# Gathers of the last token group in rows of three, each row behind the landing of the one before

## The chip, the cores and the metric

The kernel runs on one core of a Trainium2 chip. The metric is the device time of one execution in microseconds (us). Engines are named as in the profile: PE is the matrix engine (PEld its weight loads), DVE the vector engine, ACT the scalar engine, POOL the GpSimd engine, SP the sync engine, which here only issues DMAs.

## The reference, cut to what matters

Two transformer layers with pre-normalisation run over 2048 tokens of 128 channels. Each layer is an attention and a mixture of experts. The change lies in the second layer's attention, which for each query takes the 64 latest keys and 32 more that an index score picks:

```python
x = x + _L0_attn_ref(_layernorm(x), ...)     # 16 heads over all 2048 keys
x = x + _L0_ffn_ref(_layernorm(x), ...)      # 16 experts, 4 of them weighted in
x = x + _L1_attn_ref(_layernorm(x), ...)     # sparse attention, below
x = x + _L1_ffn_ref(_layernorm(x), ...)      # shared and routed experts
# in _L1_attn_ref
c_kv = x @ W_dkv
I = jnp.einsum('bths,h->bts', relu(einsum(q_i, k_i)), idx_w)
I = jnp.where(local[None], jnp.inf, I)       # the latest LW = 64 keys always
I = jnp.where(causal[None], -jnp.inf, I)
_, idx = jax.lax.top_k(I, 96)
key_c = (c_kv @ W_uk)[bi, idx]
value = (c_kv @ W_uv)[bi, idx]
kr_sel = (x @ W_kr)[bi, idx]                 # turned by rotary angles of the rank in the top k
attn = softmax(scores)
out = einsum(attn, value) @ W_out
```

So each of the 2048 queries has 32 key rows that only its own scores name, and these rows must be fetched one by one by index.

## The kernel before, in words

The tokens stand in 16 tiles of 128, in four groups of four tiles. The first layer's attention (`run`, from L422) is one long pipeline over 32 units, eight for each group of queries. When the eight units of a group are done, the rest of the network for that group, `follow(g)`, is a generator: `experts0`, `attention1`, `experts1`. For groups 0 to 2 it is drawn upon in small pieces by `advance`, so that its instructions stand between those of the next group's units. For group 3 there is no next group: at L503 `self.alone` is set, and `follow(3)` (tiles 12 to 15) runs by itself until the kernel's end. This is the tail, from about 2450 us on.

In `attention1` the compressed keys of the group (32 columns) and its rotary keys (32 columns) go to `table` in DRAM, one row of 64 floats (256 bytes) for each token. Then, for each tile n:

- `index_scores(n)` (L792): PE products, ACT relu and DVE sums make the score vector v (128 queries by up to 1984 keys).
- `choose(n)` (L824): four rounds on DVE of max, max_index and match_replace give 32 indices for each query in ix, which L842 turns into ixT. Then come 32 gathers, `gather(g)`: each is one indirect DMA issued by POOL (L853) that fetches, for one column of ixT, 128 rows of the table into slot 2·(g mod 16) + g div 16 of the tile kv, which has 32 slots. kv has three buffers, so tile 15's gathers write where tile 12's were.
- `queries(n)` (L866): the queries, their softplus and their rotation; eight small loads of the window's keys, issued by SP.
- `attend(n)` (L913): DVE rotates the 32 key columns of kv in two halves (L97, L100, L103, L104, all from the helper `rotate`). The first half reads slots 0 to 15, that is gathers 0 to 7 and 16 to 23; the second half the others, so it needs the last gather. PE transposes the result (L932), makes the scores (L942, L950, L956); then softmax (L962 to L974), the transposes of the weights (L983), the values (L991, L998), and the output product (L1012), added to xr at L1013.

While another group runs (`alone` false), the gathers are put in a list, `pay` issues one or two at a time between other work, and the branch at L847 puts them into rows of three: once three have been issued, POOL first copies one element column of each of the three landed slots into a small tile `at` (L850), which can only be done when those gathers have landed, and then issues the next. In the last group (`alone` true) that branch is not taken; L862 issues all 32 gathers of a tile one after the other. The list `issued` is made once for each group, so it runs on over the group's four tiles.

The order of the program in the tail is written at L1030 to L1042: index_scores and choose of tiles 12 and 13, then index_scores and choose of 14 beside queries and attend of 12, the same for 15 beside 13, then queries and attend of 14 and of 15. The framework plans the final order on each engine from this program order and its own estimate of when things are ready; instructions given to `keep_in_program_order` (the gathers, the copies, the first two steps of a rotation) stay in the order in which they are written. Each engine then runs its instructions strictly in that order. After `attend(15)` comes `experts1` for the group, which begins with the layernorm of all four tiles, and the output.

Of the kernel before, what the change touches and what calls it, by code (L numbers as in the profile page):

```python
# [106 lines left out]
class Program:  # L107
# [617 lines left out]
    def attention1(self, sc, g):  # L725
# [58 lines left out]
        gathers, issued, vs, chosen, qTs = [], [], {}, {}, {}  # L784

        def pay(us):

            for _ in range(min(len(gathers), max(1, round(us / 1.8)))):
                gathers.pop(0)[1]()
            return us  # L790
# [33 lines left out]
        def choose(n):  # L824

            v = vs.pop(n)
            us = v.shape[1] / 950 + 0.1
            ix = sm.tile([P, RK], U32, tag="ix", name=f"ix{n}")  # L830
            ixT = sm.tile([P, RK], U32, tag="ixT", name=f"ixT{n}", bufs=4)
            kv = sm.tile([P, RK, 64], F32, tag="kv", name=f"kv{n}", bufs=3)
            for r in range(RK // 8):
                m8 = sm.tile([P, 8], F32, tag="m8", name=f"m8_{n}_{r}")
                nc.vector.max(m8, v)
                yield pay(us)
                nc.vector.max_index(ix[:, 8 * r : 8 * r + 8], m8, v)
                yield pay(us)
                if r < RK // 8 - 1:
                    nc.vector.match_replace(v, m8, v, GONE)  # L840
                    yield pay(us)
            nc.vector.transpose(ixT, ix)  # L842

            def gather(g):
                def go():

                    if not self.alone and len(issued) == 3:  # L847
                        at = sm.tile([P, 3], F32, tag="at", name=f"at{n}_{g}")
                        for i, slot in enumerate(issued):
                            tc.keep_in_program_order(nc.gpsimd.tensor_copy(at[:, i : i + 1], slot))  # L850
                        issued.clear()
                    tc.keep_in_program_order(
                        nc.gpsimd.indirect_dma_start(  # L853
                            out=kv[:, 2 * (g % 16) + g // 16, :], out_offset=None, in_=table[0 : P * (n + 1), :],
                            in_offset=bass.IndirectOffsetOnAxis(ap=ixT[:, g : g + 1], axis=0),
                        )
                    )
                    issued.append(kv[:, 2 * (g % 16) + g // 16, 0:1])
                return go

            gathers.extend((n, gather(g)) for g in range(32))
            while self.alone and gathers:  # L862
                gathers.pop(0)[1]()
            chosen[n] = kv
# [381 lines left out]
```

## Time and profile before

| | |
|---|---|
| runs shown: median (lowest to highest) | 2804.27 us (2803.74 to 2807.57), 3 runs |
| profiled execution: time / span | 2803.35 us / 2801.6 us |
| mean granted clock of PE over the span | 0.942 |
| busy, of the span: PE / DVE / ACT / POOL | 91% / 60% / 64% / 24% |
| DMA_INDIRECT at L853, whole kernel | 512, 506.3 us busy, 989 ns mean |
| of these in the tail | 128, first start 2576.6 us, last start 2744.9 us |
| COPY at L850, whole kernel | 378 (groups 0 to 2 only), 77.8 us busy, 211 ns mean |
| other POOL instructions from 2480 us on | none |

The span is the time from the first instruction to the last on the core; the execution's own time is 1.75 us longer. The busy shares are means over stages with different limits: over the first 2400 us PE is nearly always busy, while in the tail, in the last two or three of forty equal slices of the span, PE is at five to seven tenths and POOL at seven. A row in a timeline gives the start, the duration, the engine, the line and operation, what is written from what, and in brackets the idle time before and the instruction or transfer that ended it.

### The profile page before, as it was taken

Reading aid. Unit: us, or ns where it says so; the run is one execution under the profiler, and the core shown is the slowest. Engines: PE = TensorE matmul, PEld = TensorE weight load, DVE = VectorE, ACT = ScalarE, POOL = GpSimd, SP = SyncE. Lnnn points to the kernel's source line nnn. Section 1 sums busy time; section 2 is a strip of 40 time slices with the busy share of each in tenths; the row PEclk is TensorE's granted clock in tenths of the full one; section 3 lists DMA queues with packets and bytes.
Section 4 is the critical chain, followed back from the end, with each engine's and each line's share of the span. In section 5 each row is a group of like instructions: output and inputs, shape, how many; then the busy total and the mean of one; then the engine's idle time right before and its main releaser. Section 6 shows DMA issues by size and latency. Waiting matters only on the chain. (4 is left out here: it accounts for less than half of the span.)

```text
span 2801.6 us, 39304 instructions
## 1 busy us (share of the span) xinstructions
PE 2538.6 (91%) x13452; PEld 1170.6 (42%) x13452; DVE 1670.8 (60%) x4650; ACT 1789.8 (64%) x4192; POOL 671.3 (24%) x964
## 2 busy tenths in 40 slices
PE   6999999999989999999989999999989999975566
PEld 3444444434434444434334444444433444442344
DVE  7655554565664454566685455466687654288863
ACT  3777778866666776766666677755665677533343
POOL 2111110000166610000166630000055460001771
PEclk9999999999999999999999999999999999986566
DMA  4322221111111111111121111111011120100111
GB/s 134 88 61 61 57 61 46 44 43 50 30 43 48 48 37 55 49 45 38 33 48 43 48 33 59 42 43 48 25 38 37 37 49 16 63 23 12 26 26 38
DMA packets 98103, 127.79 MB, mean 46 GB/s; under 512 B 31344, under 2 KB 49776, under 8 KB 97904
## 3 DMA queue, kind: packets, MB, share of 16 engines
q1 hardware_dynamic: 81520, 108.48, 13.8%
q0 software_dynamic: 16384, 16.81, 2.9%
q8 instruction: 106, 1.74, 0.3%
q14 instruction: 93, 0.76, 0.1%
HBM read 115.26 MB, written 9.96 MB: 45 GB/s over the span
## 5 line engine op out<-in xcount | busy, mean ns | idle before, releaser
L340 ACT ACTIVATE neg<-neg,mx 128x512 f32<-128x512 f32 x1024 | 729.8, 714 | 305.3 <-DVE neg L329 296.6
L329 DVE TENSOR_SCALAR_CACHE_REDUCE neg<-pa 128x512 f32<-128x512 f32 x1024 | 657.7, 686 | 428.1 <-PE pa L323 423.4
L390 ACT ACTIVATE e<-pb 128x512 f32<-128x512 f32 x1024 | 550.4, 595 | 293.0 <-PE pb L386 280.1
L384 PE MATMUL pb<-q,kb 64*128 64x512 f32 x2048 | 638.8, 628 | 8.5 <-DVE t_q L302 5.2
L323 PE MATMUL pa<-ka,q 64*128 64x512 f32 x2048 | 597.7, 621 | 21.9 <-ACT e L390 15.0
L853 POOL DMA_INDIRECT kv<-table,ixT x512 | 506.3, 989 | 425.3 <-DVE v L804 266.9
L399 PE MATMUL po<-e,ckv 128*64 128x512 f32 x2048 | 511.7, 612 | 0.0
L323 PEld LDWEIGHTS pa<-ka,q 64*128 64x128 f32 x2048 | 245.2, 190 | 227.0 <-issue 101.7
L303 POOL TENSOR_TENSOR q<-t_q 128x512 f32<-128x512 f32 x32 | 40.8, 1274 | 1206.3 <-DVE t_q L302 1106.7
L384 PEld LDWEIGHTS pb<-q,kb 64*128 64x128 f32 x2048 | 225.4, 190 | 210.8 <-issue 106.1
L386 PE MATMUL pb<-mrow,onesb 64*128 64x512 bf16 x1024 | 252.5, 383 | 6.8 <-ACT mrow L375 6.8
L399 PEld LDWEIGHTS po<-e,ckv 128*64 128x64 f32 x2048 | 126.9, 137 | 301.0 <-issue 283.6
L340 ACT ACTIVATION_READ_ACCUMULATOR neg<-neg,mx 128x1 f32 x1024 | 192.3, 188 | 0.0
L802 PE MATMUL pi<-kiT,qiT 64*128 64x512 f32 (+4 forms) x320 | 110.0, 610 | 26.1 <-DVE v L804 14.7
L386 PEld LDWEIGHTS <-onesb 64*128 64x128 bf16 x1024 | 69.2, 96 | 127.4 <-issue 119.6
L418 DVE SCALAR_TENSOR_TENSOR xr<-pp,rs,xr 128x128 f32<-128x128 f32 x256 | 72.2, 344 | 82.6 <-PE pp L415 69.4
L850 POOL COPY at<-kv 128x1 f32<-128x1 f32 x378 | 77.8, 211 | 174.3 <-DMA kv<-table,ixT 168.8
L721 DVE SCALAR_TENSOR_TENSOR hb<-thb,zb 128x512 f32<-128x512 f32 x64 | 44.3, 692 | 113.2 <-ACT zb L719 113.1
L808 DVE SCALAR_TENSOR_TENSOR v<-rl,iw_sb,v 128x512 f32<-128x512 f32 (+4 forms) x120 | 76.4, 642 | 51.1 <-ACT rl L807 46.7
L966 ACT ACTIVATE e<-pl,mx 128x208 f32<-128x208 f32 x128 | 54.3, 429 | 81.1 <-DVE mx L963 79.5
L303 POOL TENSOR_TENSOR kst<-t_k 128x512 f32<-128x512 f32 x32 | 41.0, 1283 | 264.0 <-DVE t_k L302 168.2
L962 DVE TENSOR_REDUCE mx<-pl 128x2 f32<-128x416 f32 x64 | 37.7, 590 | 100.3 <-PE pl L956 99.9
(276 smaller groups left out, 2859.0 us busy)
## 6 DMA issues: line engine op xcount, KB each, us to landing
ka<-kd SPq DMA_DIRECT2D x128, 256.0 KB, 3.6
kb<-kd SPq DMA_DIRECT2D x128, 256.0 KB, 3.7
wb<-in_wx SPq DMA_DIRECT2D x64, 192.0 KB, 2.4
kd<-kst SPq DMA_DIRECT2D x32, 256.0 KB, 2.3
kv<-table,ixT POOLq DMA_INDIRECT x512, 2.5
wd<-in_wx SPq DMA_DIRECT2D x40, 192.0 KB, 3.7
csk<-in_cs SPq DMA_DIRECT2D x4, 512.0 KB, 6.7
csq<-in_cs SPq DMA_DIRECT2D x4, 512.0 KB
```

The costliest lines, as they stand in the source:

```text
L303: nc.gpsimd.tensor_tensor(dst, t[:, 0, :], t[:, 1, :], ALU.add)
L323: nc.tensor.matmul(ps[h], q[rows, qt * P : qt * P + P], k[rows, :], start=True, stop=True)
L329: nc.vector.tensor_scalar(t, ps[h], -1.0, None, ALU.mult, ALU.min, accum_out=mx[at])
L340: nc.scalar.activation(t, t, AF.Exp, bias=mx[at], scale=-1.0, accum_out=su[at])
L384: nc.tensor.matmul(ps[h], k[rows, c], q[rows, :], start=True, stop=False)
L386: nc.tensor.matmul(ps[h], self.onesb[rows, :], mrow[rows, :], start=False, stop=True)
L390: nc.scalar.activation(e[:, h, :], ps[h], AF.Exp)
L399: nc.tensor.matmul(self.pos[u][cols, :], self.ckv[:, kb, :], e[:, h, :], start=(kb == 0), stop=(kb == NT - 1))
L802: nc.tensor.matmul(pi[:, : hi - lo], qiT[h // 2][rows, q], kiT[rows, lo:hi], start=True, stop=True)
L808: nc.vector.scalar_tensor_tensor(v[:, lo:hi], rl[:, : hi - lo], w["iw"][:, h : h + 1], v[:, lo:hi], ALU.mult, ALU.add)
L850: tc.keep_in_program_order(nc.gpsimd.tensor_copy(at[:, i : i + 1], slot))
L853: nc.gpsimd.indirect_dma_start(out=kv[:, 2 * (g % 16) + g // 16, :], out_offset=None, in_=table[0 : P * (n + 1), :], in_offset=bass.Indire ...
```

## The change

One condition falls. The branch that makes rows of three was taken only while another group ran beside; now it is taken in the last group as well:

```diff
@@ -844,7 +844,7 @@
             def gather(g):
                 def go():
 
-                    if not self.alone and len(issued) == 3:
+                    if len(issued) == 3:
                         at = sm.tile([P, 3], F32, tag="at", name=f"at{n}_{g}")
                         for i, slot in enumerate(issued):
                             tc.keep_in_program_order(nc.gpsimd.tensor_copy(at[:, i : i + 1], slot))
                         issued.clear()
```

What follows in `go` (the gather itself and `issued.append`) is as it was. The 128 gathers of the tail get the copies before the 4th, the 7th and so on: 42 times, three copies each. The rows run on over the borders of tiles, since 32 is not a multiple of three. Nothing of groups 0 to 2 is changed, and no value that the kernel computes.

## The prediction

> **What bounds the kernel now.** I read the page's slices first, then the gathers' own line in the tail, then the timelines of POOL and DVE there. The slices say where to look:
>
> ```profile
> PE   6999999999989999999989999999989999975566
> POOL 2111110000166610000166630000055460001771
> PEclk9999999999999999999999999999999999986566
> ```
>
> The edit touches only the last group, which runs alone. There PE is idle three to five tenths, so the 91% of the whole span says nothing about it, and POOL, at 24% overall, is at seven tenths for two slices of 70 us. The line of the gathers, for the window from 2480 us on:
>
> ```profile
> L853 POOL DMA_INDIRECT kv<-table,ixT x128: 942/947/3062, 2576.6 to 2744.9; - x128
> ...
>   DVE v L804: 255.5, 1
>   issue: 40.1, 123
> ...
> DMA to landing us min/median/max: 2.3/2.4/4.5
> ```
>
> 128 gathers start over 168.3 us. POOL waited once for the first (255.5 us, nothing to do yet) and otherwise nearly only for its own issue: 40.1/123 = 0.33 us between one and the next. The timelines of POOL and of DVE at the end of the tail:
>
> ```profile
> 2700.58 0.94 POOL L853 DMA_INDIRECT kv<-table,ixT  x1 [0.30 <-issue]
> 2701.83 0.95 POOL L853 DMA_INDIRECT kv<-table,ixT  x1 [0.30 <-issue]
> 2705.70 0.94 POOL L853 DMA_INDIRECT kv<-table,ixT  x1 [2.92 <-issue]
> 2706.94 0.95 POOL L853 DMA_INDIRECT kv<-table,ixT  x1 [0.30 <-issue]
> ...
> 2744.92 0.95 POOL L853 DMA_INDIRECT kv<-table,ixT  x1 [0.30 <-issue]
> ```
> ```profile
> 2704.75 0.21 DVE L842 STREAM_TRANSPOSE ixT<-ix 128x32 uint32<-128x32 uint32 x1
> ...
> 2745.76 0.69 DVE L97 TENSOR_TENSOR w<-kv,cs 128x512 f32<-128x512 f32 x1 [1.44 <-DMA kv<-table,ixT]
> ...
> 2747.77 0.68 DVE L97 TENSOR_TENSOR w<-kv,cs 128x512 f32<-128x512 f32 x1
> ```
>
> A gather every 1.25 us, four tiles in one unbroken train; the only gap, 2.92 us at 2705, is tile 15's train waiting for its indices (L842). The last gather starts at 2744.92 and lands 2.4 us later, at 2747.3; attend(15)'s second rotation, which needs it, starts at 2747.77. From there 53.8 us of attend(15) and experts1 lead to the end of the span. So POOL's train sets the end of the tail to within half a microsecond: whatever is added to it comes out at the end, but for the 2.6 us of the gap above the usual 0.30.
>
> **What the change adds.** Nothing is removed. 128 gathers get floor(127/3) = 42 rows of copies. What such a row costs is shown by the earlier groups, which run the very code (POOL timeline, group 0):
>
> ```profile
> 758.26 0.95 POOL L853 DMA_INDIRECT kv<-table,ixT  x1 [0.31 <-issue]
> 759.21 0.48 POOL L850 COPY at<-kv 128x1 f32<-128x1 f32 x2
> 760.61 0.18 POOL L850 COPY at<-kv 128x1 f32<-128x1 f32 x1 [0.93 <-DMA kv<-table,ixT]
> 760.94 0.97 POOL L853 DMA_INDIRECT kv<-table,ixT  x1
> 762.22 0.95 POOL L853 DMA_INDIRECT kv<-table,ixT  x1 [0.30 <-issue]
> 763.47 0.95 POOL L853 DMA_INDIRECT kv<-table,ixT  x1 [0.30 <-issue]
> ```
>
> The third gather starts at 758.26; the last copy waits for its landing, 2.35 us later; the next gather starts at 760.94. The step is 2.68 us where it would be 1.25: 1.43 more. The next row starts 763.47 + 2.79 later, 1.54 more. Two of the three copies run while the third transfer is under way, so they are free; the price is landing plus one copy plus its step to the next gather: 2.4 + 0.18 + 0.15 - 1.25 = 1.48 us with the tail's median landing.
>
> Over all rows of groups 0 to 2 whose step holds nothing but copies (123 in the POOL timelines) the median step is 2.85 and the mean 3.05 without the four above 4.5 us; other gathers step by 1.30 in the mean. That makes 1.55 to 1.75. Those groups ran beside key loads at 40 to 50 GB/s, the tail's train makes 26 GB/s in all; but the tail's gathers are disturbed just as often (mean step (2744.92 - 2576.58 - 2.62)/127 = 1.305 against an undisturbed 1.25). Ends: 1.43 (the best-placed row above) and 1.79 (mean row start to row start of 5.70, less three steps of 1.305). I take 1.60, between the tail's own landing and the busier groups' mean. Sum: 42 x 1.60 = **67.2 us** on POOL, ends 60.1 and 75.2.
>
> A page has a price for the same wait: the Trainium skill, "DMA: Bandwidth & Descriptors", section "Anatomy of one DMA — SWDGE (gpsimd) path", puts a DMA issued by GpSimd at 2.0 us plus bytes/436e3; for 32 KB that is an estimate of 2.08 us. By it a row would cost 1.16 us and the rows 48.7; the trace's 2.4 us decides.
>
> **What waits behind.** Behind a waiting copy on POOL stand only gathers; POOL has no other work from 2480 us on. Those who wait for the gathers are the rotations on DVE, and behind them in DVE's order parts of choose. By 1.305 a gather and 1.60 a row, a tile's train is 32 x 1.305 + 10.67 x 1.60 = 58.8 us. It ends at 2635.4 for tile 12, 2694.2 for 13, 2753.0 for 14.
> - Tile 12's second rotation, before at 2622.13 after a stall of 5.38, waits until about 2636.5, 14.4 later. choose(14) behind it, done at 2651.8 before, is done at 2666.2; POOL wants it at 2694.2. 28 to spare.
> - Tile 13's second rotation moves from 2674.05 to 2695.3; choose(15) from 2704.96 to 2726.2, wanted at 2753.0. 27 to spare, so the gap of 2.92 before tile 15 is gone: **-2.6 us**.
> - attend(14) starts its second rotation at 2754.1 instead of 2714.77; with queries(15), which ended at 2744.3, that work took 29.6 us and is done by 2783.7, before tile 15's last landing. Hidden.
> - kv's buffer for tile 15 is free when attend(12) has read it, some 30 us after its rotation: by about 2667, before 2753.0.
> - The eight loads of the window keys are SP's and aren't queued behind anything that waits here: 0. The three-column tile `at` is only written, by POOL in order: 0.
>
> **At the end.** The last gather starts at 2576.6 + 127 x 1.305 + 42 x 1.60 = 2809.5 and lands at 2811.9. The second rotation starts there, 64.1 us after its 2747.77 (the 0.45 of slack is used up). The first half and its transposes will then be long done: before, the second half's transposes started at 2750.50, 0.64 after their rotation's end at 2749.86, behind the first half's work: **-0.6**. But PE will have stood idle before. In the same place for tile 14 the granted clock was 0.57 from 2710 to 2715 and 1.00 from 2715 to 2720: after a pause PE runs some 3.7 us (the sixteen query transposes from 2710.70) at half speed. attend(15) had paid that on its query transposes; now it pays on the second half's work: 3.7 us that do 1.85 us of it, **+1.9** (0 if the first half keeps PE warm, 4 if softmax's pauses are lengthened too).
>
> Sum: 67.2 - 2.6 - 0.5 - 0.6 + 1.9 = **65.4 us**. The profiled execution would go from a span of 2801.6 to 2867.0 and from 2803.35 to 2868.8. It was 0.9 below the median of the runs shown, so against the median: 2804.3 + 65.4 = 2869.7, say **2870 us**. With the ends of the row price and of the clock: 60.1 - 3.7 + 0 = 56 to 75.2 - 3.7 + 4 = 76, so 2860 to 2880.
>
> **Rivals.**
> 1. *The slack swallows three tiles.* If the trains of tiles 12 to 14 were hidden behind choose, only tile 15's 10.67 rows would count: 10.67 x 1.6 = 17, so 2821. For it: DVE is above nine tenths from 2580 to 2600, and it made the 2.92 gap. Against it: one gap of 2.92 in 168 us is no slack. Chance 0.05.
> 2. *DVE's order starves POOL.* The framework plans anew with the slower POOL; were choose(15) put wholly behind attend(13) (rotation at 2695; 27 us of attend, for tile 14 2712.76 to 2739.51; 37 us of choose, for tile 15 2667.84 to 2704.96), its indices would come at 2759 instead of 2726, 6 us after POOL wants them; with choose(14) likewise and rotations mis-set by a row or two, 15 to 35 us more: 2885 to 2905. For it: the order before had a stall of 5.38 because a rotation was put too early. Against: 27 us of room, twice. Chance 0.11.
> 3. *Not slower: the wait was there anyway.* If gathers beyond three in flight only queued behind one another, holding them back would cost nothing, and the long ones (up to 3.06 us) might go: at most 128 x (1.305 - 1.25) = 7 us of gain, minus the gap's 2.6 that would reappear, 2800 to 2804. It decides from the point where a landing comes within the next issue, 1.25 us after its start; the trace has none below 2.2, and the landing doesn't grow along the unbroken train (median 2.4, against 2.5 in all). Chance 0.04.
> 4. *The edit does nothing*: `issued` is appended to in both cases, so it reaches three in the last group; nothing for it, under 0.01, counted with 3.
>
> **How the numbers follow.** The forecast has 0.80: 2870, its own range 2860 to 2880. Range for eight in ten: 2857 to 2886, which reaches a little below the ends and to the near end of rival 2. A change within 0.2% (5.6 us) can't be told from none here. Slower: 0.80 + 0.11 + 0.05 = 0.96; rival 3 is split, 0.02 same and 0.02 faster.
>
> **What would show it.** 504 copies at L850 in all, 126 of them after 2570 us; rows of 5.3 to 5.7 us in the tail's POOL timeline, the last copy of each ended by a landing; the last gather's start near 2809 with no gap before tile 15; the second rotation of tile 15 ended by that landing; some 54 us from there to the end. I'd be wrong if the tail's landings in rows of three were clearly shorter than 2.3 us or the mean row above 5.8, if POOL waits for L842 in tile 14 or 15, or if something other than kv releases attend(15).

## The result and the profile after

| | before | after |
|---|---|---|
| median (lowest to highest) | 2804.01 us (2802.11 to 2807.57), 4 runs | 2874.0 us (2871.22 to 2878.28), 4 runs |
| ratio, 95% interval | 1 | 1.0247 [1.0229, 1.0264] |
| profiled execution: time / span | 2803.35 / 2801.6 us | 2878.28 / 2876.5 us |

The change makes the kernel 70.0 us slower, where +65.4 was forecast (2870). The profiled execution of after is the slowest of its four, so its span shows a difference of 74.9.

The 40 slices of after, on its page:

```profile
PE   6999999999989999999989999999899999763546
POOL 2111100000366600000456500000344620006660
```

POOL's work in the tail was two slices at seven tenths; it is three at six. It works less densely for longer, and PE in the last slices is at three to six tenths. The gathers' line L853 from 2480 us on, and then the copies' line L850 in the same window:

```profile
L853 POOL DMA_INDIRECT kv<-table,ixT x128: 940/947/3067, 2580.5 to 2813.9; - x128
...
  issue: 14.8, 48
  DMA kv<-table,ixT: 11.6, 38
...
DMA to landing us min/median/max: 2.3/2.4/4.5
```
```profile
L850 POOL COPY at<-kv x126: 173/184/732, 2585.1 to 2812.3; 128x1 f32<-128x1 f32 x126
...
  DMA kv<-table,ixT: 46.2, 46
```

The 126 copies are there, and POOL sat idle 46.2 us ahead of them for landings. A landing takes what it took before, 2.4 us in the median: holding gathers back has not made them quicker. The train, first start to last, is 233.4 us where it was 168.3. POOL's timeline at the border to tile 15 and at the end of the train (start, duration, what, and in brackets the idle time before and its releaser):

```profile
2757.05 0.34 POOL L850 COPY at<-kv 128x1 f32<-128x1 f32 x2
2758.55 0.18 POOL L850 COPY at<-kv 128x1 f32<-128x1 f32 x1 [1.16 <-DMA kv<-table,ixT]
2759.24 0.97 POOL L853 DMA_INDIRECT kv<-table,ixT  x1 [0.51 <-issue]
...
2809.92 0.94 POOL L853 DMA_INDIRECT kv<-table,ixT  x1 [0.30 <-DMA kv<-table,ixT]
2810.87 0.36 POOL L850 COPY at<-kv 128x1 f32<-128x1 f32 x2
2812.31 0.18 POOL L850 COPY at<-kv 128x1 f32<-128x1 f32 x1 [1.08 <-DMA kv<-table,ixT]
2812.64 0.97 POOL L853 DMA_INDIRECT kv<-table,ixT  x1
2813.91 0.94 POOL L853 DMA_INDIRECT kv<-table,ixT  x1 [0.31 <-issue]
```

Tile 15's first gather starts at 2759.24, 0.51 us after the copy before it: the gap of 2.92 is gone. The row at 2809.92 is as in groups 0 to 2: two copies free, the third 2.39 us after its gather's start, the next gather 2.72 after it. DVE's timeline for attend(15), after and then before:

```profile
2816.43 0.69 DVE L97 TENSOR_TENSOR w<-kv,cs 128x512 f32<-128x512 f32 x1 [12.86 <-DMA kv<-table,ixT]
...
2830.71 0.20 DVE L971 RECIPROCAL ri<-su 128x8 f32<-128x8 f32 x1 [1.07 <-ACT e L966]
...
2843.43 0.29 DVE L1013 TENSOR_TENSOR xr<-xr,pj 128x128 f32<-128x128 f32 x1 [12.52 <-PE pj L1012]
```
```profile
2758.97 0.20 DVE L971 RECIPROCAL ri<-su 128x8 f32<-128x8 f32 x1 [1.07 <-ACT e L966]
...
2771.69 0.29 DVE L1013 TENSOR_TENSOR xr<-xr,pj 128x128 f32<-128x128 f32 x1 [12.52 <-PE pj L1012]
```

DVE stood still for 12.86 us until the last landing released the second rotation. From there to the reciprocal it is 14.28 us, where it was 11.20 (2758.97 less 2747.77); from the reciprocal to L1013 12.72 in both. The 74.9 us of the two spans:

| stretch | before | after | more | forecast |
|---|---|---|---|---|
| start of the span to the tail's first gather | 2576.6 | 2580.5 | +3.9 | 0 |
| first gather to tile 15's second rotation | 171.2 | 236.0 | +64.8 | +64.1 |
| of it the rows, (233.4 - 165.7) / 42 each | | 1.61 | +67.7 | +67.2 |
| rotation to reciprocal (L971) | 11.20 | 14.28 | +3.1 | +1.3 for the three |
| reciprocal to the addition (L1013) | 12.72 | 12.72 | 0 | |
| addition to the end of the span | 29.9 | 33.1 | +3.2 | |

165.7 is the train of before without the excess of its gap, 168.34 - 2.62; it is the base for every price of a row below.

### The profile page after: what moved, and what is told of

It reads as the page before. It is cut to its first block, busy times and chain, and to the rows that moved or that the text cites. A ratio compares the mean times of both kernels' runs of the same rounds, so it can differ in the third digit from the quotient of the medians.

```text
span 2876.5 us, 39470 instructions
## 1 busy us (share of the span) xinstructions
PE 2549.5 (89%) x13452; PEld 1181.5 (41%) x13452; DVE 1672.1 (58%) x4650; ACT 1790.3 (62%) x4192; POOL 696.0 (24%) x1090
## 5 line engine op out<-in xcount | busy, mean ns | idle before, releaser
L853 POOL DMA_INDIRECT kv<-table,ixT x512 | 504.6, 986 | 416.1 <-DVE v L804 267.0
L850 POOL COPY at<-kv 128x1 f32<-128x1 f32 x504 | 104.2, 214 | 211.7 <-DMA kv<-table,ixT 207.9
L932 PE MATMUL ptr<-ident,kv 128*128 128x128 f32 x256 | 45.8, 322 | 101.6 <-DVE kv L104 57.3
```

The lines of the kernel that those rows point to most:

```text
L853: nc.gpsimd.indirect_dma_start(out=kv[:, 2 * (g % 16) + g // 16, :], out_offset=None, in_=table[0 : P * (n + 1), :], in_offset=bass.Indire ...
```

## The experiments

The theory (T): the landing wait costs about 1.6 us for each row, and because POOL's train sets the end, every row comes out there. The rivals: slack swallows the rows of tiles 12 to 14 (R1), DVE's order starves POOL (R2), or the wait was there anyway (R3). The experiments ran on three chips, and this matters: the unchanged kernel of before takes 2807.87 us (10 runs) on the first, much as in the runs of the result (2804.01, their chip is not on record), but 2908.86 (20 runs) on the second and 2920.26 (25 runs) on the third. A total is therefore set only beside before's on its own chip. Most expectations had counted from 2804; on the second and third chip none of those totals came out, not even as a difference from before there (e1 to e4 and e10 to e12), and these runs are read by their trains of gathers. The tail's timelines can be compared across chips where nothing disturbs them (the train of after is 235.4 us on the first chip and 236.2 on the third); what disturbs them is shown under rows in tile 15 alone.

### The same kernel again: e5 (first chip), e9 (third chip)

The kernel of after itself.

> The changed kernel as it is, for a second profile. The train of gathers, first start to last start, should again be 231 to 236 us; the start of the train may differ by some microseconds with what lies before it. The stretch from tile 15's second rotation to the end of the span was 60.1 us; if part of it is the phase in which the matrix engine's clock rises in the last experts, it lies anywhere from 56 to 61.

> The changed kernel as it is, beside the other three. Where the matrix engine is fed in time during an unbroken train: 65 to 75 us above the kernel before, as seen twice. On a chip where the unbroken train is accompanied by matrix instructions that come late (as in the first four runs, where the kernel before took 2909 us), rows should relieve that: the train of about 235 us again, but no more than some 10 us above the kernel before, since there the one-copy kernel, whose train is 17 us longer, was 14 us above it.

On the first chip 2877.62 us (4 runs), ratio 1.0265 [1.0236, 1.0294]: the result repeats. The profile's train runs 235.4 us from 2577.6; rotation to reciprocal is 14.28 once more (as in e4, e9 and e12, within 0.01), but from the reciprocal to the addition it is 11.42 instead of 12.72, and from the addition to the end 30.2 instead of 33.1. On the third chip the train is nearly the same, 236.2 us with no gap, yet the kernel takes 2914.12 (10 runs) against 2920.26, ratio 0.9977 [0.995, 1.0005]: no difference that can be told. In its own stretch the change costs what it did on the first chip, so before must lose about as much in the tail there; no profile of before on that chip shows where.

### What a row is made of: e7, e1, e2 and e11

Rows of one (e7, first chip); one copy for each row of three (e1, second chip); rows of three copied three gathers late, so that nothing has to be waited for (e2 on the second, e11 on the third chip). The edits to after:

```diff
-                    if len(issued) == 3:
+                    if len(issued) == (1 if self.alone else 3):
```
```diff
-                        for i, slot in enumerate(issued):
+                        for i, slot in enumerate(issued[2:] if self.alone else issued):
```
```diff
-                    if len(issued) == 3:
+                    if len(issued) == (6 if self.alone else 3):
...
-                        for i, slot in enumerate(issued):
+                        for i, slot in enumerate(issued[:3]):
...
-                        issued.clear()
+                        del issued[:3]
```

> The changed kernel, but rows of one in the last group: 127 rows, each gather waits for the one before. By the price of a row, 1.48 to 1.6 us: 188 to 203 us, less 2.6, and 3 to 6 for the matrix engine: 2992 to 3010.

> The changed kernel, but in the last group only the third slot of a row is copied: 42 copies in the tail instead of 126, the wait for the third landing stays. If the landing sets the price of a row (about 1.6 us), the two other copies run in its shadow and the time stays at that of the changed kernel, 2870 to 2878 us. Rival: if the copies' own work on POOL sets it, two thirds of the added time go: some 43 of 65 us, so about 2828.

> The changed kernel, but in the last group a row's copies stand behind the issue of the next row: the same three copies in a row, of gathers that were issued at least three issues (3.75 us) before and, with a landing of 2.4 us, have landed. If the wait for the landing is the price, it goes, and what is left is the copies' own time, no longer in a shadow: three of 0.15 to 0.2 us and a step, 0.5 to 0.8 us a row, 41 rows, 20 to 33 us, less 2.6 for the gap before tile 15: 2822 to 2838. Rival, that POOL turning from a gather to a copy and back costs by itself: near 2870.

> Copies one row behind, once more: 41 rows of copies that wait for nothing. In the first look the step with three such copies was 1.53 us against 1.25 to 1.28 without. If the wait for the landing is nearly all of the price: 41 x 0.28 = 11 us, less 2.6, and 0 to 3 for the matrix engine: 2812 to 2817 where the kernel before takes 2804. If the copies themselves were the price: near 2870.

| | chip | time, ratio to its before | train | price of a row |
|---|---|---|---|---|
| e7, 127 rows of one | first | 3056.71, 1.0892 [1.0861, 1.0923] | 423.2 | (423.2 - 165.7) / 127 = 2.03 |
| e1, 42 rows, one copy | second | 2923.05, 1.0046 [1.0024, 1.0067] | 252.0 | (252.0 - 165.7) / 42 = 2.05 |
| e2, 41 rows late | second | 2892.63, 0.9933 [0.9912, 0.9954] | 181.2 without two waits for L842 | 0.38 |
| e11, 41 rows late | third | 2914.42, 0.9991 [0.9965, 1.0017] | 183.6 without two such waits | 0.44 |

Three copies without a wait cost about 0.4 us, with the wait 1.6: three quarters of the price is the landing. Both late runs lie between the 0.28 that e11 expected and the 0.5 to 0.8 of e2. Two expectations missed in the price itself. The rows of one came out above 3010, because a lone copy makes a row dearer than three copies do, 2.03 against 1.61; e1, expected at the price of after, shows the same on another chip, so taking copies away saves nothing. POOL's timeline in e7:

```profile
2702.01 0.98 POOL L853 DMA_INDIRECT kv<-table,ixT  x1 [0.47 <-issue]
2704.68 0.18 POOL L850 COPY at<-kv 128x1 f32<-128x1 f32 x1 [1.70 <-DMA kv<-table,ixT]
2705.34 0.98 POOL L853 DMA_INDIRECT kv<-table,ixT  x1 [0.47 <-issue]
```

The copy starts 2.67 us after the gather, and the next gather 0.47 after the copy's end; in the row of three shown for after these are 2.39 and 0.15. The medians over all rows are 2.60 and 0.47 in e7, 2.55 and 0.47 in e1, 2.41 and 0.14 in after. Why, the runs don't show.

### Half as many rows: e3 (second chip), e10 (third chip)

```diff
-                    if len(issued) == 3:
-                        at = sm.tile([P, 3], F32, tag="at", name=f"at{n}_{g}")
+                    if len(issued) == (6 if self.alone else 3):
+                        at = sm.tile([P, 6], F32, tag="at", name=f"at{n}_{g}")
```

> The changed kernel, but rows of six in the last group: 21 rows instead of 42, 126 copies as before. A price for each row, whatever it holds: 21 x 1.6 = 34 us, less 2.6, and 1 to 6 us for a colder matrix engine at the end: 2836 to 2843. Rival, a price for each copy: near 2870.

> Rows of six in the last group (21 rows, 126 copies), once more. Train: 127 x 1.305 + 21 x 1.6 = 199 us (200.1 in the first look). Where nothing else is late: 31 us less 0.5 and 1 to 6 for the matrix engine, 2836 to 2843 beside 2804. A price for each copy instead would give near 2870.

The trains are 200.1 and 201.5 us: (200.1 - 165.7) / 21 = 1.64 and 1.70 a row, with twice as many copies in each. The price goes by rows, not by copies or gathers, as T has it. In time rows of six beat before on both of these chips: 2875.74 against 2908.86, ratio 0.988 [0.9863, 0.9898], and 2874.26 against 2920.26, 0.9851 [0.9803, 0.9899]. They were not run on the first chip; an estimate from the trains, less the gap of 2.6, is 2807.9 + 21 x 1.64 - 2.6 = 2840, slower than before.

### Rows in tile 15 alone: e4 (second chip), e12 (third chip)

```diff
-                    if len(issued) == 3:
+                    if (not self.alone or n == NT - 1) and len(issued) == 3:
...
-                    issued.append(kv[:, 2 * (g % 16) + g // 16, 0:1])
+                    if not self.alone or n == NT - 1:
+                        issued.append(kv[:, 2 * (g % 16) + g // 16, 0:1])
```

> Rows of three in the last tile alone (10 rows), tiles 12 to 14 in one unbroken train as before the change. If every row of the train comes out at the end: 10 x 1.6 = 16 us, less half a microsecond of slack, and 1 to 6 us for the matrix engine: 2820 to 2827. Rival, that the rows of tiles 12 to 14 were hidden behind other work and only the last tile's count: near 2870.

> Rows of three in tile 15 alone (10 rows), once more: 10 x 1.6 = 16 us, less 0.5, and 1 to 6 for the matrix engine: 2820 to 2827 where the kernel before takes 2804, if every row comes out at the end. If only the last tile's rows counted, near 2870.

This was to decide between T and R1 by the total, and by the total it decides nothing: 2908.2, ratio 1.0006 [0.9976, 1.0035], and 2912.73, 0.9971 [0.9947, 0.9995]. The trains tell why. That of e4 is 227.4 us, and two waits that before, as profiled, doesn't have stand in it. POOL's timeline of e4, from the last gather of tile 13 on:

```profile
2688.53 0.95 POOL L853 DMA_INDIRECT kv<-table,ixT  x1 [0.30 <-issue]
2714.92 0.95 POOL L853 DMA_INDIRECT kv<-table,ixT  x1 [25.44 <-DVE ixT L842]
...
2777.16 0.94 POOL L853 DMA_INDIRECT kv<-table,ixT  x1 [19.30 <-issue]
```

POOL waits 25.44 us for tile 14's indices and 19.30 before tile 15's. Without these (each less the usual 0.30), 227.4 - 25.1 - 19.0 = 183.3: tile 15's rows added 17.6. Tile 15's own 31 steps give 15.1: 2832.76 - 2777.16 = 55.6 us, less 31 x 1.305. The list `issued` starts empty at tile 15 here, so there are 10 rows, and 10 x 1.6 = 16. The waits come from elsewhere, which PE's timeline in the same kernel shows, while POOL still gathers and just after (L957 there is L956 of after; the edit adds a line):

```profile
2676.41 0.37 PE L957 MATMUL pl<-kr,qT 64*32 64x128 f32 x1 [2.43 <-issue]
2679.20 0.37 PE L957 MATMUL pl<-kr,qT 64*32 64x128 f32 x1 [2.43 <-issue]
2682.01 0.37 PE L957 MATMUL pl<-kr,qT 64*32 64x128 f32 x1 [2.43 <-issue]
...
2696.01 1.10 PE L957 MATMUL pl<-kr,qT 64*32 64x128 f32 x15 [0.33 <-issue]
```

Matmuls of 0.37 us follow one another every 2.8 us, each after 2.43 us of waiting for nothing that the profile shows; some 7 us after the last gather of the train has been issued, fifteen of them run within 1.10. DVE's timeline of e4 has the consequence:

```profile
2696.09 1.09 DVE L963 TENSOR_REDUCE mx<-pl 128x2 f32<-128x416 f32 x2 [36.99 <-remote]
...
2714.45 0.20 DVE L842 STREAM_TRANSPOSE ixT<-ix 128x32 uint32<-128x32 uint32 x1
```

DVE stands still for 36.99 us ahead of the max that reads those products; attend(12) is late by that, the rest of choose(14) stands behind it in DVE's order, and POOL waits for choose(14). In e12 the two waits are 28.63 and 22.49 us. In before and after on the runs shown, in after on the third chip (e9) and in e1 on the second, no such runs of steps stand in the tail, and in e8 on the first chip neither, though its train is unbroken; with rows of six (e3, e10) there are some, of up to 1.15 us of waiting each. So on the second and third chip an unbroken train goes with late instructions on PE, and rows of three go without; that fits before being slower there and after not. Before itself was not profiled on these chips, so for it this is argued.

### Choose first: e8 (first chip)

Could before be made faster instead? Here DVE's order in the tail is written out, choose(14) ahead of attend(12), and kv has a fourth buffer. The edit to before:

```diff
-            for m in range(n, n + 4):
-                if m < n + 2:
+            with tc.manual_schedule(engines={mybir.EngineType.DVE}):
+                for m in range(n, n + 2):
                     yield from index_scores(m)
                     yield from choose(m)
-                else:
-                    yield from beside(1, index_scores(m), queries(m - 2))
-                    yield from beside(3, choose(m), attend(m - 2))
+                yield from beside(1, index_scores(n + 2), queries(n))
+                yield from choose(n + 2)
+                yield from beside(1, index_scores(n + 3), queries(n + 1))
+                yield from beside(3, choose(n + 3), attend(n))
+            yield from attend(n + 1)
```

> The kernel before the change, with the last group's work on DVE kept in an order written by hand: tile 13's score sums stand behind tile 12's choice instead of between its steps, tiles 13 and 14 are chosen before any attend, kv has a fourth buffer. If the unbroken train of gathers sets the end, all that starts it earlier comes out at the end: eleven foreign steps of 0.65 us leave tile 12's choice, so the train starts some 7 us earlier, and choices that come in time keep it unbroken: 2790 to 2800. Rival, that DVE is the bound as soon as POOL is not: no change, 2804, or slower.

2823.44 us (7 runs), ratio 1.0054 [1.004, 1.0069]: half a percent slower, where 2790 to 2800 was expected; the rival named there holds. The train is unbroken, 2574.6 to 2742.4. But the last rotation, in DVE's timeline:

```profile
2771.01 0.69 DVE L97 TENSOR_TENSOR w<-kv,cs 128x512 f32<-128x512 f32 x1 [1.45 <-PE ptq L905]
...
2773.02 0.68 DVE L97 TENSOR_TENSOR w<-kv,cs 128x512 f32<-128x512 f32 x1
```

It starts 30.6 us after the last gather and waits for no landing: with the attends pushed back, the chain of DVE, ACT and PE, and no longer POOL, leads to the end. In before, the two bounds lie within half a microsecond.

### The clock at the end: e6 (first chip)

After, with twelve matmuls whose result nothing reads behind the first half's transposes of tile 15, so that PE works while it waits for the last landing:

```diff
+                if n == NT - 1 and q == 1:
+                    pw = self.x("pw", [P, 512])
+                    for _ in range(12):
+                        nc.tensor.matmul(
+                            pw, ident, kv[:, 0:8, :].rearrange("p a b -> p (a b)"), start=True, stop=True
+                        )
```

> The changed kernel with twelve products on the matrix engine that nobody reads, placed between the first and the second half of tile 15's transposes, where it stands idle for 13 us. If the clock is what made the stretch from tile 15's second rotation to its reciprocal 14.3 us instead of 11.2, the granted clock stays near 1.0 there and the stretch falls to 11 to 12.5; the time falls by some 2 to 3 us. Rival, that the order of the instructions made it longer: it stays at 14 or more.

PE's timeline of after around the second rotation, and then that of e6 (L962 there is L956 of after):

```profile
2806.96 1.08 PE L956 MATMUL pl<-kr,qT 64*32 64x128 f32 x16
2818.95 1.97 PE L932 MATMUL ptr<-ident,kv 128*128 128x128 f32 x8 [10.91 <-DVE kv L104]
...
2827.70 1.08 PE L956 MATMUL pl<-kr,qT 64*32 64x128 f32 x16
```
```profile
2818.62 11.74 PE L937 MATMUL pw<-kv,ident 128*128 128x512 f32 x24
2832.09 1.09 PE L932 MATMUL ptr<-ident,kv 128*128 128x128 f32 x8 [1.73 <-DVE kv L104]
...
2833.89 0.64 PE L962 MATMUL pl<-kr,qT 64*32 64x128 f32 x16
```

Eight transposes take 1.97 us in after and 1.09 in e6; a group of sixteen score products (L956) takes 1.08 in after and 0.64 in e6. Rotation to reciprocal falls from 14.28 to 11.30: the cause is PE's clock, which in e6's windows is granted at 0.50 up to 2820 and at 1.00 from 2822 on. That 11.30 is so near the 11.20 of before is partly chance. In before and e6 all four groups of scores stand behind the second rotation; in after the first of them (the row at 2806.96 ends it) ran before it, during the wait. A group takes 1.45 us at full clock in e6, so an estimate for after at full clock is 11.30 - 1.45 = 9.85, and the slow clock costs some 4.4 us of the 14.28. The total, 2876.71 (4 runs) against 2877.62 of e5, shows less than 3, but the runs of each spread over 10 us or more, so the total neither confirms nor denies it.

## Why the prediction was right, and where it was off

**The bound.** POOL's train sets the end: the second rotation of tile 15 is released by the last landing in after, e5 and e9, and what the rows add to the train is in the span. Right.

**The price of a row.** 1.60 forecast, 1.61 measured, 1.66 in e5 and 1.68 in e9. It is made mostly of the wait for the landing: without the wait (e2, e11) a row costs 0.4. The estimate by the formula of the Trainium skill, "DMA: Bandwidth & Descriptors", section "Anatomy of one DMA — SWDGE (gpsimd) path", which gave 1.16 for a row and 48.7 us in all, was too low. The trace's own median landing of 2.4 us gave 1.48, and the choice of 1.60, between that and the earlier groups' mean, came out: the last copy of a row starts 2.41 us after its gather in the median of after and 2.55 in the mean, and a sum goes by the mean.

**The gap.** -2.6 forecast; 0.51 us is left between the last copy and tile 15's first gather, so the gap is gone. DVE had room: choose(15) is done at 2733.1, 26 us before tile 15's first gather (27 forecast), and R2 (0.11) did not happen. Tile 12's second rotation starts at 2641.5 instead of 2636.5 as forecast, mostly because the train itself starts 3.9 later.

**R1, slack for three tiles.** Refuted by the train of after: all 42 rows are in the 64.8 us, and POOL has no gap in which they could have vanished. The experiment meant for it was spoilt in its total by the chips, though its train shows the 10 rows of tile 15 at 15 to 18 us, near their price.

**R3, not slower.** In the result and in e5 it is wrong, and so is its mechanism: the landing is 2.4 us with and without rows. On the third chip its outcome holds, after and before are level, by something else that was not in the prediction.

**The term that was mis-sized.** "At the end" was forecast at -0.6 + 1.9 = +1.3 and is +6.2 in the profiled execution, +2.1 in e5. The step that failed is the clock: the prediction took the duration of PE's slow phase from tile 14, 3.7 us that do 1.85 us of work. In before, PE's query transposes of tile 15 are that phase:

```profile
2743.70 3.68 PE L905 MATMUL ptq<-ident,qq 128*128 128x128 f32 x16 [4.23 <-ACT qq L897]
```

The windows of after from 2815 us on, and one of before at the same place of attend(15) (columns: length; busy time and count of PE, weight loads, DVE, ACT, POOL; granted clock; DMA share; GB/s):

```profile
2815.00:2820.00 5.00, 1.05 (x5) 1.05 (x6) 2.54 (x6) 0.93 (x4) 0.00 (x0) 0.50 0.03 7
2820.00:2825.00 5.00, 5.00 (x31) 3.05 (x29) 0.34 (x1) 1.18 (x3) 0.00 (x0) 0.50 0.01 3
2825.00:2830.00 5.00, 3.78 (x39) 2.21 (x38) 1.95 (x6) 2.15 (x9) 0.00 (x0) 0.50 0.00 0
```
```profile
2750.00:2755.00 5.00, 5.00 (x68) 3.36 (x67) 1.62 (x5) 2.68 (x9) 0.00 (x0) 1.00 0.02 3
```

In after the clock stays at 0.50 until the scores are done, although PE works from 2818.95 to 2828.78 without a break: 9.8 us, not 3.7. So the whole stretch is paid at half speed, by the estimate under e6 some +4.4 where +1.9 was forecast. The -0.6 was too small as well: with one of four score groups done during the wait, by the same estimate 11.20 - 9.85, some -1.3. The two errors partly cancel, to +3.1. The Trainium skill, "TensorE: Matmul & The Clock Gate", Part 1, lets the full clock return after about 3.4 us of sustained work; this trace disagrees for these matmuls. In before, 3.7 us of 128-row transposes stood ahead of the scores and in e6 the unread 128-row products did, and the clock rose in both; in after there are 2 us of such transposes and then mostly products of 64 rows. That the rows are what counts is a guess that no run isolates.

The other +3.2, behind L1013, is not steady: 33.1 us in after, 30.2 in e5, 30.3 in e6, 29.9 in before. It is the clock again: in after PE is granted 0.90 and 0.76 in the windows from 2860 to 2870, in experts1, where before, as far from the end, has 1.00; the 32 matmuls of L1102 take 4.55 us for 3.68, and in e5 3.68. The +3.9 ahead of the train lies in code that is the same in both (+1.0 in e5). Neither comes back at that size in e5, so both look like scatter between executions, of which the profiled one drew both. That e5 comes to +2.1 at the end, near the forecast +1.3, is luck in part: its +3.1 is offset by the 1.3 us that its reciprocal to addition is shorter. The median of the runs lies 4 us above the forecast, within its own range of 2860 to 2880.

## What to carry to other kernels

A wait for a transfer cost here its landing less what the engine would have issued meanwhile, once for each row and not for each transfer; whether it reaches the end is told by whether the waiting engine releases the last consumer of the stage. Price it from the same code elsewhere in the trace, and count the rows. And set a kernel only beside the before of its own chip: here the same two kernels differ by 2.5% on one and by nothing that can be told on another.

## What the runs showed of the hardware that was not expected

- **Chips differ.** The unchanged kernel takes 2807.87, 2908.86 and 2920.26 us on three chips, and after 2877.62 on the first and 2914.12 on the third. Part lies ahead of the tail: the tail's first gather starts at 2576.6 in before and 2580.5 in after as shown, at 2572.8 to 2591.3 in the kernels on the first chip, and at 2604.8 to 2623.2 in those on the second and third. For after that part is all of it: 38.6 us between e5 and e9, where the medians differ by 36.5. For e4 and e12 there are the waits in the tail besides. A lower clock throughout is not the cause: in windows of 500 us up to 2000 us it is 0.97 to 0.99 in e5 and in e9. Each chip had its runs on one occasion, so chip and occasion can't be told apart.
- **Late instructions.** On those chips PE steps by 2.8 us through a part of an unbroken train (e4), with waits that the profile can put down to nothing but issue. What in the chip causes it stays open: no run isolates it.
- **A lone copy is dearer than three.** A row costs 2.03 (e7) and 2.05 us (e1) with one copy, 1.61 with three.
- **PE's clock** stayed at half for 9.8 us of unbroken matmuls in after; rotation to reciprocal took the same 14.28 us in e4, e5, e9 and e12.
